# Graph layers on one core: scores of gathered tiles taken earlier and pinned in order, the diagonal's and `mixed`'s evictions moved later

## The chip, the core and the metric

The kernel runs on one core of a Trainium2 chip. The metric is device time in microseconds (us), from the start of the program to its end. One more execution was taken with the hardware profiler; its span and its rows are what is read below. Engines are named as in the profile: PE is TensorE (matrix products), DVE VectorE, ACT ScalarE, POOL GpSimd, SP SyncE. PEld is the loading of weights, beside PE.

## The reference

There are 64 graphs of 256 nodes with 256 features, and all share one weighted adjacency matrix `adj` (256 x 256, about 3% of it not zero, symmetric in its pattern, with a full diagonal). Four layers follow each other: 0, 1 and 3 are of one kind, and 2 is attention. The weights differ from layer to layer.

```python
def gnn(h, adj, W1, b1, W2, b2, Wa, ba, Wm, bm, beta1, beta2, beta3):   # layers 0, 1, 3
    pre_u = einsum('bud,dk->buk', h, W1[:d])
    pre_v = einsum('bvd,dk->bvk', h, W1[d:])
    hidden = relu(pre_u[:, :, None, :] + pre_v[:, None, :, :] + b1)
    S = sigmoid(einsum('buvk,ko->buvo', hidden, W2)[..., 0] + b2[0])
    a = einsum('buv,bud->bvd', S * adj, h)
    m = einsum('uv,bud->bvd', adj, h) * h
    return beta1 * h + beta2 * (a @ Wa + ba) + beta3 * (m @ Wm + bm)

def attention(x, adj, W1, W2, b2, bias2):                               # layer 2
    feats = einsum('bni,oi->bno', x, W1)
    f1 = einsum('bno,o->bn', feats, W2) + b2[0]
    coefs = softmax(leaky_relu(f1[:, :, None] + f1[:, None, :]) + adj, axis=-1)
    return einsum('bij,bjo->bio', coefs, feats) + bias2 + x
```

The score `S[u, v]` is wanted only where `adj[u, v]` is not zero. For each such edge it is a sum over 256 features of `relu(pre_u[u] + pre_v[v] + b1) * W2`.

## The kernel before, in words

**Edges in slots.** The edges off the diagonal are put into 16 blocks of 128 slots, and what does not fit goes into a rest (`left`). A block is named (k, m, i): half k of row block m, quarter i of the columns. For each slot the row pre_u[u] + pre_v[v] + b1 is wanted, for two graphs g at once. It comes in one of three ways.

- Eight blocks (`FAST`) are *made* by TensorE: `pick` (a 0/1 matrix) times `pre` (copies of rows of `pu` and `pv` that ScalarE lays out, `rows_u` L751 and `rows_v` L760), into one of three PSUM tiles `ga` (L697).
- Eight blocks (`FETCHED`) and `left` are *gathered* by POOL's indirect DMAs (L742, in the order `FETCHES`). SP first writes `pu` and `pv` as tables to DRAM (L630). For each block one gather takes the rows of `tableu`, and a second one adds those of `tablev` on top. A stage has 18 gathers. The first six (`AHEAD`) are issued in `before`, the others in `scores`.
- The diagonal (u = v) needs no gather: `own` is pu + pv, added by DVE out of PSUM (L636, four 128x256 adds a stage).

**Scores.** `rated` is one DVE instruction per block and graph (L661, tile `junk`): relu, times W2, summed to a column of `raw`. `rated_all` then turns a run of columns into scores on ACT (tanh at L681, an add of 1 at L682), and four DVE products write them as matrices `rm` (L689). It is called twice a stage: for `EARLY` (the rest, the diagonal and all blocks of m = 0, with the product `ro` for the rest on ACT, L684) and for `LATE` (all blocks of m = 1, in `end`, when all else of the stage is issued).

**Back to the graph.** `early` makes the matrix `sa` from the diagonal and the rest: PE products of `ro` and `guo` (L771) into two PSUM tiles, and four DVE steps (L775). `spread` adds the blocks: for m = 0 and then m = 1, PE products of `rm` and `gu` (L787) and one DVE add (L789). `finish` then has the products `sa,h` (L281, evicted to `aT` by ACT, L344), those with the weights Wm and Wa (L366, or L352 in the last layer), DVE's sum into `hT` or `h` (L369, L356), and transposes (L287). `mixed` has the products `adj,h` (L281) and DVE's products with `hT` into `mT` (L316). `before` has the products of `hT` with W1 (L625), `pu` on ACT (L626) and `pv` on DVE (L627). `attention` has products with `qb` (L401) and `w2q` (L407), the exponentials `e` on ACT, transposes of `e` that ACT copies to SBUF (`ident,e`, L287), and the products `f,logits` (L448).

**Two streams.** Stream a has 16 pairs of graphs, stream b the other 16. While the scores of one stream's layer are taken (the *heavy* side), the other stream does all its work between two score phases (the *light* side): `after` (= `spread` and `finish`), attention if it is due, and `before` of the next layer, which ends with `mixed`. `beside` weaves them: the light side is a generator, and with each step it yields a number p, or a pair (p, f): so many made tiles, and so many steps of `got` (gathered tiles), are issued there. `REST_OF_IT` issues all that remains, so everything from there on (`early`, L771) stands at the end of the stage, just before `mixed`'s `adj,h`.

**Stages.** There are 96 score phases. Six make a cycle for four graphs: the scores are those of layer 0 of a, layer 0 of b, layer 1 of a, layer 1 of b, layer 3 of a, layer 3 of b, and attention is on the light side of the fourth and the fifth. Where the text cuts a stage at the first `adj,h` matmul, the `LATE` rating and `spread` of the scores just finished fall into the first microseconds of the next stage.

**What sets the order.** A tile scheduler orders each engine's instructions by a model of when their operands come; `tc.issue_after(x)` makes an instruction stand behind x on its engine. Before the change it is used for the gathers (each behind the last) and for the rows of `pre` (behind the last stage's rating, `past`). PSUM has five `ps` tiles for everything but `ga`.

Of the kernel before, what the change touches and what calls it, by code (L numbers as in the profile page):

```python
# [9 lines left out]
FP = mybir.dt.float32  # L10
# [5 lines left out]
P = 128  # L16
# [16 lines left out]
FAST = [(0, 0, 2), (0, 0, 3)] + [(0, 1, i) for i in range(4)] + [(1, 0, 2), (1, 0, 3)]  # L33
# [4 lines left out]
FETCHES += [(-1, 0), (2, 1), (4, 0), (3, 1), (5, 0), (-1, 1), (6, 0), (4, 1), (7, 0), (5, 1), (6, 1), (7, 1)]  # L38

AHEAD = 6  # L40

# [16 lines left out]
def quarter(q):  # L58
    return slice(q * 64, (q + 1) * 64)

# [18 lines left out]
def adj_seq_kernel(ctx: ExitStack, tc: tile.TileContext, a: dict, out: bass.AP):  # L79
# [15 lines left out]
    mm = nc.tensor.matmul  # L95
# [36 lines left out]
    def z_weights(l):  # L132
        for kept, n, beta in ((wm, "Wm", "beta3"), (wa, "Wa", "beta2")):
            kept[l] = const.tile([P, 2, D], FP, name=l + n)
            nc.sync.dma_start(out=kept[l], in_=a[l + n].rearrange("(c p) e -> p c e", p=P))
            nc.scalar.mul(kept[l], kept[l], sca(l + beta))
        zbias[l] = const.tile([P, 2], FP, name=l + "zbias")
        zb = const.tile([P, 2], FP, name=l + "zb")
        nc.vector.tensor_scalar(zb, vecs[:, VEC[l + "ba"], :], sca(l + "beta2"), None, ALU.mult)
        nc.vector.scalar_tensor_tensor(  # L140
# [5 lines left out]
    for l in GNN:  # L146
        halfb2[l] = const.tile([P, 1], FP, name=l + "halfb2")
        nc.vector.tensor_scalar(halfb2[l], sca(l + "b2"), 0.5, None, ALU.mult)
    twob2 = const.tile([P, 1], FP, name="twob2")
    nc.vector.tensor_scalar(twob2, sca("L2_gnn_b2"), 2.0, None, ALU.mult)  # L150
# [7 lines left out]
    def counts(keep, pool, pc):  # L158
# [3 lines left out]
        nc.vector.tensor_scalar(mask, adj, 0.0, None, ALU.not_equal)  # L162
# [6 lines left out]
        nc.vector.tensor_tensor_scan(upto.rearrange("p s v -> p (s v)"), flat, flat, 0.0, ALU.add, ALU.bypass)  # L169
        past = pool.tile([P, 8], FP, name="past")  # L170
        nc.vector.memset(past, 0.0)
        nc.vector.tensor_copy(past[:, 1:8], upto[:, 0:7, 63])
        deg = pool.tile([P, 8], FP, name="deg")
        nc.vector.tensor_tensor(deg, upto[:, :, 63], past, ALU.subtract)
# [17 lines left out]
        nc.vector.tensor_copy(first, t[:, 0:8])  # L192
        last = keep.tile([P, 8], FP, name="last")
        nc.vector.tensor_tensor(last, first, deg, ALU.add)

        over = pool.tile([P, 8], FP, name="over")
        nc.vector.tensor_scalar(over, t[:, 8:16], -128.0, 0.0, ALU.add, ALU.max)
        begin = keep.tile([P, 9], FP, name="begin")
        nc.vector.memset(begin, 0.0)
        nc.vector.tensor_tensor_scan(begin[:, 1:9], over, over, 0.0, ALU.add, ALU.bypass)  # L200
        t = pc()
        mm(out=t[:, 0:1], lhsT=other, rhs=begin[:, 8:9], start=True, stop=True)
        nc.vector.tensor_scalar(begin, begin, t[:, 0:1], None, ALU.add)
        number = keep.tile([P, 8, 64], FP, name="number")
        shift = pool.tile([P, 8], FP, name="shift")
        nc.vector.tensor_tensor(shift, first, past, ALU.subtract)
        nc.vector.tensor_tensor(number, upto, shift.unsqueeze(2).to_broadcast([P, 8, 64]), ALU.add)
# [752 lines left out]
```

## Time and profile before

| | us |
|---|---|
| median of 3 runs | 3524.88 |
| lowest, highest | 3524.08, 3527.32 |
| the profiled execution, its own time | 3531.84 |
| its span, first to last instruction | 3529.9 |
| PE busy | 3446.7 |
| DVE busy | 2605.4 |
| POOL busy | 2227.1 |
| ACT busy | 1599.5 |
| granted TensorE clock, mean | 0.992 |

The busy times are sums over instructions. A matmul's record ends at a modelled time, so PE's busy time also covers short holes between matmuls; where a hole matters, the starts of the records are compared. A 512-column product in fp32 shows as two records, and so on; the counts behind an x are records. In the waits, "PE ps L787 <- DVE rm L689: 29.4, 31, 4.9" reads: PE waited before L787 for a DVE instruction of L689, 29.4 us in all, 31 times, 4.9 at the longest.

### The profile page before, as it was taken

To read this page: it belongs to the slowest core of one execution; us is meant where nothing else is said; L and a number is where in the kernel's file an instruction comes from. 1 tells how busy PE (TensorE), PEld (TensorE's weight loads), DVE (VectorE), ACT (ScalarE), POOL (GpSimd) and SP (SyncE) were. 2 spreads that over 40 slices of the span, in tenths; PEclk is the share of its full clock that TensorE was granted. 3 is DMA by queue.
4 is the path that set the end of the run, shared out by engine and by line. 5 is a ranking of instruction groups with operands and counts; after the bars stand their busy time and mean duration, and the time that the engine had idled before them with its cause. 6 is when DMAs were issued, how large, how long until landed. Compare 5 with 4: busy or idle time off the path is not lost.

```text
span 3529.9 us, 48385 instructions
## 1 busy us (share of the span) xinstructions
PE 3446.7 (98%) x14328; PEld 2106.0 (60%) x14328; DVE 2605.4 (74%) x10584; ACT 1599.5 (45%) x2929; POOL 2227.1 (63%) x1754
## 2 busy tenths in 40 slices
PE   6999999999999999999999999999999999999998
PEld 3566565656656566565666656556565665656655
DVE  5777686777867777777777777768677787777776
ACT  2444444444444444444545445444444444444452
POOL 3747667576665757667576675766757566675754
PEclk7999999999999999999999999999999999999999
DMA  5768777687777867778687776867768677786865
GB/s 148 163 141 192 155 178 168 160 182 155 182 157 170 176 146 188 150 181 181 145 191 161 178 172 151 188 153 185 163 162 179 150 187 157 176 177 146 192 150 114
DMA packets 274733, 587.25 MB, mean 166 GB/s; under 512 B 37024, under 2 KB 54304, under 8 KB 274464
## 3 DMA queue, kind: packets, MB, share of 16 engines
q0 software_dynamic: 190464, 427.93, 60.7%
q1 hardware_dynamic: 82416, 154.96, 12.7%
q8 instruction: 116, 1.90, 0.2%
q10 hardware_dynamic: 1584, 1.20, 0.1%
q14 instruction: 153, 1.25, 0.1%
HBM read 466.51 MB, written 117.44 MB: 165 GB/s over the span
## 4 chain that ended last, share of the span: by engine, by line
PE 72%; DVE 11%; DMA 5%; POOL 5%; issue 5%; ACT 2%; ACTq 0%; POOLq 0%; DVEq 0%
PE ga L697 14%; PE ps L281 13%; PE ps L625 13%; PE ps L366 10%; PE ps L352 5%; POOL fetched L742 4%; PE ps L787 4%; PE ps L448 3%; DVE junk L661 3%; PE ps L407 3%; DMA fetched<-tablev,ids_v 3%; DVE rm L689 3%; PE ps L287 2%; DVE sa L775 2%; PE ps L401 2%
## 5 line engine op out<-in xcount | busy, mean ns | idle before, releaser
L742 POOL DMA_INDIRECT fetched<-tablev,ids_v x768 | 1210.7, 1576 | 355.3 <-issue 232.6
L742 POOL DMA_INDIRECT fetched<-tableu,ids_u x768 | 764.8, 996 | 824.1 <-DMA tableu<-pu 594.0
L697 PE MATMUL ga<-pre,pick 128*128 128x512 f32 x1536 | 769.7, 605 | 11.7 <-DVE junk L661 8.4
L625 PE MATMUL ps<-L_gnn_w,hT 128*128 128x512 f32 x1536 | 695.5, 596 | 5.8 <-DMA hT<-in_xT_dram 5.8
L661 DVE SCALAR_TENSOR_TENSOR junk<-ga,L_gnn_w2row 128x256 f32<-128x256 f32 x1536 | 582.7, 418 | 134.6 <-PE ga L697 122.6
L661 DVE SCALAR_TENSOR_TENSOR junk<-fetched,L_gnn_w2row 128x256 f32<-128x256 f32 x1536 | 595.1, 417 | 35.1 <-DMA fetched<-tablev,ids_v 35.0
L760 ACT COPY pre<-pv 64x512 f32<-64x512 f32 x768 | 473.5, 616 | 108.8 <-DVE pv L627 86.7
L625 PEld LDWEIGHTS ps<-L_gnn_w,hT 128*128 128x128 f32 x1536 | 285.1, 191 | 334.7 <-issue 313.6
L751 ACT COPY pre<-pu 64x1024 f32<-64x1024 f32 x384 | 392.9, 1039 | 3.9
L369 DVE TENSOR_TENSOR hT<-hb,ps 128x512 f32<-128x512 f32 x128 | 88.0, 687 | 412.9 <-PE ps L366 412.9
L697 PEld LDWEIGHTS ga<-pre,pick 128*128 128x128 f32 x1536 | 274.7, 191 | 179.2 <-issue 122.4
L281 PE MATMUL ps<-adj,h 128*128 128x256 f32 x1536 | 358.7, 386 | 11.1 <-DVE own L636 8.0
L281 PE MATMUL ps<-sa,h 128*128 128x256 f32 x1536 | 362.4, 385 | 3.7 <-issue 2.9
L281 PEld LDWEIGHTS ps<-sa,h 128*128 128x128 f32 x1536 | 290.3, 192 | 109.0 <-issue 46.2
L626 ACT COPY pu<-ps 128x256 f32<-128x256 f32 x384 | 142.4, 371 | 466.9 <-PE ps L625 443.2
L281 PEld LDWEIGHTS ps<-adj,h 128*128 128x128 f32 x1536 | 283.4, 190 | 80.0 <-issue 36.8
L330 ACT ACTIVATE hb<-hT,L_gnn_zbias,scas 128x512 f32<-128x512 f32 x128 | 97.4, 807 | 450.3 <-DVE hT L369 356.7
L689 DVE TENSOR_TENSOR rm<-gva,val 128x256 f32<-128x256 f32 x768 | 279.0, 417 | 9.7 <-ACT val L682 7.2
L787 PEld LDWEIGHTS ps<-rm,gu 128*64 128x64 f32 x3072 | 172.4, 137 | 139.2 <-PE ps L281 55.4
L787 PE MATMUL ps<-rm,gu 128*64 128x128 f32 x3072 | 215.9, 280 | 30.9 <-DVE rm L689 29.4
L344 ACT COPY aT<-ps 128x512 f32<-128x512 f32 x192 | 112.6, 586 | 293.2 <-PE ps L281 250.3
L366 PE MATMUL ps<-mT,L_gnn_Wm 128*128 128x512 f32 x512 | 240.6, 592 | 0.0
(155 smaller groups left out, 4200.2 us busy)
## 6 DMA issues: line engine op xcount, KB each, us to landing
tableu<-pu SPq DMA_DIRECT2D x192, 256.0 KB
tablev<-pv SPq DMA_DIRECT2D x192, 256.0 KB
hT<-in_xT_dram SPq DMA_DIRECT2D x32, 512.0 KB
h<-in_x_dram SPq DMA_DIRECT2D x64, 256.0 KB
out_dram<-h SPq DMA_DIRECT2D x64, 256.0 KB
fetched<-tableu,ids_u POOLq DMA_INDIRECT x768
fetched<-tablev,ids_v POOLq DMA_INDIRECT x768
L_gnn_w<-in_L_gnn_W_dram SPq DMA_DIRECT2D x6, 256.0 KB
```

The lines of the kernel that those rows point to most:

```text
L281: mm(out=o[:, m, :], lhsT=lhs[:, c, blk(m)], rhs=rhs[:, c, :], start=c == 0, stop=c == 1)
L352: mm(out=z[:, m, :], lhsT=y[:, c, g, blk(m)], rhs=w[:, c, :], start=j == 0 and c == 0, stop=j == 1 and c == 1)
L366: mm(out=z, lhsT=w[:, c, blk(m)], rhs=y[:, c], start=j == 0 and c == 0, stop=j == 1 and c == 1)
L625: mm(out=t, lhsT=hT[:, c, g, blk(m)], rhs=w1[l][:, c], start=c == 0, stop=c == 1)
L626: nc.scalar.copy(pu[:, m, g, :], t[:, 0, :])
L661: nc.vector.scalar_tensor_tensor(junk, t, 0.0, w2row[l], ALU.max, ALU.mult, accum_out=raw[:, i : i + 1])
L689: nc.vector.tensor_tensor(rm[:, k, ms, g, :], gva[:, k, ms, :], val[:, i : i + 4].unsqueeze(2).to_broadcast([P, 4, 64]), ALU.mult)
L697: mm(out=t, lhsT=pick[:, k, 4 * m + i, :], rhs=pre[:, n], start=True, stop=True)
L742: this = nc.gpsimd.indirect_dma_start(out=to, out_offset=None, in_=rows, in_offset=bass.IndirectOffsetOnAxis(ap=ids, axis=0), compute_op=( ...
L751: nc.scalar.copy(st["pre"][h, f : f + n], st["pu"][h, m].rearrange("p g d -> p (g d)").unsqueeze(1).to_broadcast([64, n, 2 * D]),)
L760: nc.scalar.copy(st["pre"][halves[1 - k], n], st["pv"][halves[i % 2], i // 2].rearrange("p g d -> p (g d)"))
L787: mm(out=t[h, :, quarter(i)], lhsT=gu[:, k, 4 * m + i, :], rhs=rm[:, k, 4 * m + i], start=True, stop=True)
```

## The change

Six things are changed.

1. `FAST` lists all blocks of m = 0 first, so `EARLY` needs only the first four made tiles. The rows of `pre` follow that order.
2. In `FETCHES`, the second gather of `left` goes one place ahead.
3. The step tables are new (`STEPS`, and `steps` in `before`). `early` becomes a step of its own behind the `EARLY` rating, and in the changed kernel's program its matmuls stand in mid-stage. In the last layer the diagonal is a step of its own, at the start.
4. `Noting` keeps the last instruction that was issued on PE, DVE and ACT, and `behind` puts made tiles, scores of gathered tiles, the diagonal's adds, `rated_all`'s tanh and `early`'s instructions behind it on the same engine.
5. `own` is no longer added out of PSUM in `before` but in `itself`, from `pu` and `pv` in SBUF: two 128x512 adds a stage in place of four 128x256.
6. `mixed`'s DVE products into `mT` are kept in a list `later` and issued behind `spread`'s second add, one stage boundary on.

```diff
-FAST = [(0, 0, 2), (0, 0, 3)] + [(0, 1, i) for i in range(4)] + [(1, 0, 2), (1, 0, 3)]
+FAST = [(k, 0, i) for k in range(2) for i in (2, 3)] + [(0, 1, i) for i in range(4)]
...
-FETCHES += [(-1, 0), (2, 1), (4, 0), (3, 1), (5, 0), (-1, 1), (6, 0), (4, 1), (7, 0), (5, 1), (6, 1), (7, 1)]
+FETCHES += [(-1, 0), (2, 1), (4, 0), (3, 1), (-1, 1), (5, 0), (6, 0), (4, 1), (7, 0), (5, 1), (6, 1), (7, 1)]
...
+STEPS = {
+    GNN[0]: [(1, 1), (1, 1), (0, 1), (1, 0), (0, 1), (2, 1)],
+    GNN[1]: [(0, 0), (0, 1), (0, 1), (0, 0), (0, 1), (1, 1), (0, 0), (1, 1)],
+    LAST: [(1, 1), (1, 1), (0, 1), (0, 1), (1, 1), (1, 0)],
+}
...
+class Noting:
+    def __init__(self, engine):
+        self.engine = engine
+
+    def __getattr__(self, op):
+        def issue(*a, **k):
+            self.last = getattr(self.engine, op)(*a, **k)
+            return self.last
+        return issue
...
+    tensor, vector, scalar = Noting(nc.tensor), Noting(nc.vector), Noting(nc.scalar)
+    mm = tensor.matmul
+
+    def behind(engine):
+        return tc.issue_after(engine.last.ins)
...
-        def mixed(st, l):
+        def mixed(st, l, later=None):
...
-                nc.vector.tensor_tensor(mT[:, :, g, :], t, st["hT"][:, :, g, :], ALU.mult)
+                times = (mT[:, :, g, :], t, st["hT"][:, :, g, :], ALU.mult)
+                if later is None:
+                    vector.tensor_tensor(*times)
+                else:
+                    later.append(times)
...
-            got = {LAST: (1, 0, 1, 1), GNN[1]: (1, 1, 1, 1), GNN[0]: (0, 0, 2, 1)}[l]
-            got = dict(zip(order, got))
+            steps = {LAST: [(0, 1), (0, 1), 0, 0], GNN[1]: [0, (0, 1), (0, 1), (0, 1)], GNN[0]: [(0, 1), 0, (0, 1), (0, 1)]}[l]
...
-                nc.vector.tensor_tensor(own[:, m, g, :], t[:, 0, :], pv[:, m, g, :], ALU.add)
-                if g == 1:
-                    if m == 0:
-                        rows_u(st, 0, 2, 0, 0)
-                    rows_v(st, 2 - 2 * m, 2, 0)
-                yield 0, got[(m, g)]
+                if (m, g) == (0, 1):
+                    rows_u(st, 0, 2, 0, 0)
+                    rows_v(st, 4, 2, 0)
+                if (m, g) == (1, 1):
+                    rows_v(st, 0, 2, 0)
+                yield steps[n]
...
-            yield from mixed(st, l)
+            yield from mixed(st, l, later if past else None)
...
             def rated_all(cols, m):
-                nc.scalar.activation(val[:, cols], raw[:, cols], AF.Tanh, bias=halfb2[l], scale=0.5)
+                with behind(scalar):
+                    scalar.activation(val[:, cols], raw[:, cols], AF.Tanh, bias=halfb2[l], scale=0.5)
...
-                    mm(out=t, lhsT=pick[:, k, 4 * m + i, :], rhs=pre[:, n], start=True, stop=True)
+                    with behind(tensor):
+                        mm(out=t, lhsT=pick[:, k, 4 * m + i, :], rhs=pre[:, n], start=True, stop=True)
...
-                    if n < 2:
-                        both(own[:, n], DIAGONAL + 2 * n, DIAGONAL + 2 * n + 1)
+                    count.append(n)
                     yield
...
+            def itself(m):
+                with behind(vector):
+                    vector.tensor_tensor(*(flat(t)[:, m] for t in (own, st["pu"], st["pv"])), ALU.add)
+                both(own[:, m], DIAGONAL + 2 * m, DIAGONAL + 2 * m + 1)
...
             def got(made):
+                if l == LAST:
+                    itself(0)
+                    itself(1)
+                    yield
                 for f, block in enumerate(FETCHED):
                     if f == FIRST:
-                        for _ in made:
-                            yield
-                        rated(left, REST)
+                        while len(count) < 4:
+                            next(made)
+                        with behind(vector):
+                            rated(left, REST)
                         rated_all(EARLY, 0)
                         yield
-                    tile_scores(fetched[f], *block)
-                    if f == FIRST + 1:
                         early(st)
+                        yield
+                    if l != LAST and f < 2:
+                        itself(f)
+                    with behind(vector):
+                        tile_scores(fetched[f], *block)
                     yield
...
         def early(st):
...
-                    mm(out=sides[g][:, m, :], lhsT=guo[h, m, :], rhs=ro[h, :], start=True, stop=True)
+                    with behind(tensor):
+                        mm(out=sides[g][:, m, :], lhsT=guo[h, m, :], rhs=ro[h, :], start=True, stop=True)
...
-                    nc.vector.scalar_tensor_tensor(
+                    with behind(vector):
+                        vector.scalar_tensor_tensor(
...
         def spread(st, l):
...
-                nc.vector.tensor_tensor(sa[:, m], sa[:, m], t, ALU.add)
+                it = vector.tensor_tensor(sa[:, m], sa[:, m], t, ALU.add)
+            with tc.issue_after(it.ins):
+                while later:
+                    vector.tensor_tensor(*later.pop(0))
```

Two step values inside `attention` and the yields of `finish` (now read from `STEPS`) move by one place as well. Elsewhere `nc.vector`, `nc.scalar` and `nc.tensor` become `vector`, `scalar` and `tensor`, which issue the same instructions.

## The prediction, made blind

> **What bounds the kernel.** I read the page's busy line first, then the chain that ended last, then TensorE's waits.
>
> ```profile
> PE 3446.7 (98%) x14328; PEld 2106.0 (60%) x14328; DVE 2605.4 (74%) x10584; ACT 1599.5 (45%) x2929; POOL 2227.1 (63%) x1754
> ...
> PE 72%; DVE 11%; DMA 5%; POOL 5%; issue 5%; ACT 2%; ACTq 0%; POOLq 0%; DVEq 0%
> ```
>
> TensorE is the bound, and the change leaves it the same matmuls. Only time in which it waits can be won. Its waits by the profile:
>
> ```profile
> PE ps L787 <- DVE rm L689: 29.4, 31, 4.9
> PE ga L697 <- DVE junk L661: 8.4, 2, 7.8
> ...
> PE ps L281 <- DVE own L636: 8.0, 5, 2.6
> ...
> PE ps L771 <- ACT ro L684: 3.8, 2, 3.1
> ```
>
> The largest is `spread` (L787) waiting for the rated scores `rm`. Busy 98% hides more than this: a matmul's end is modelled, so short holes show only in the spacing. I therefore cut one cycle of six stages (four graphs; 16 cycles make the run) at the first `adj,h` matmul of each stage. These are the windows, columns as on the page; the last three are granted clock, DMA share and GB/s:
>
> ```profile
> 1575.21:1606.46 31.25, 31.25 (x138) 20.33 (x136) 25.63 (x106) 14.46 (x25) 23.98 (x19) 1.00 0.86 196
> 1606.46:1638.60 32.14, 32.14 (x130) 18.12 (x128) 24.21 (x104) 15.41 (x27) 22.21 (x18) 1.00 0.81 174
> 1638.60:1672.15 33.55, 32.34 (x130) 18.39 (x128) 24.87 (x103) 15.43 (x27) 22.77 (x18) 1.00 0.77 166
> 1672.15:1715.81 43.66, 43.08 (x183) 26.55 (x181) 32.06 (x132) 20.78 (x40) 22.04 (x18) 1.00 0.64 139
> 1715.81:1758.60 42.79, 42.79 (x182) 26.21 (x180) 32.05 (x128) 19.85 (x40) 22.68 (x19) 1.00 0.67 154
> 1758.60:1789.51 30.91, 30.91 (x139) 20.49 (x137) 22.31 (x88) 13.54 (x25) 23.71 (x20) 1.00 0.88 206
> ```
>
> I call them stages 0 to 5. Matmuls that follow without a wait are 0.429 us apart with 512 columns, 0.216 with 256. Summed so, the stages would take 30.16, 30.98, 30.98, 41.39, 41.39 and 30.16. They lose 1.1, 1.2, 2.6, 2.3, 1.4 and 0.75 us. Stage 5 waits for nothing, so about 0.75 (1.16 in the attention stages 3 and 4) is the cost of switching between operand kinds. What is left is about 5 us a cycle, and it lies in the second half of `spread`:
>
> ```profile
> 1643.11 1.09 PE L787 MATMUL ps<-rm,gu 128*64 128x128 f32 x16
> 1645.42 1.42 PE L787 MATMUL ps<-rm,gu 128*64 128x128 f32 x16 [1.21 <-DVE rm L689]
> ```
>
> ```profile
> 1763.11 1.97 PE L787 MATMUL ps<-rm,gu 128*64 128x128 f32 x32
> ```
>
> ```profile
> 1794.02 1.09 PE L787 MATMUL ps<-rm,gu 128*64 128x128 f32 x16
> 1795.04 1.98 PE L697 MATMUL ga<-pre,pick 128*128 128x512 f32 x4
> 1796.95 1.09 PE L787 MATMUL ps<-rm,gu 128*64 128x128 f32 x16
> ```
>
> Stage 2 (first fence) takes 3.66 us from the first half to the next matmul, stage 5 (second) 1.97. In stages 0 and 1 (third) the scheduler has put four made tiles between the halves: no wait, but two more switches, and the second half starts only 7.44 us into the stage.
>
> **The change, part by part.** (1) `early` leaves the stage's end. Its eight matmuls took 1.06 us there (1757.54 to 1758.60) between the last L625 and `adj,h`, and its four `sa` steps 1.64 us of VectorE at the next stage's start. Both go to mid-stage. TensorE does them all the same, so this saves nothing directly. It takes the `sa` steps (and the two `own` evictions, 0.74 us, and the two `mT` evictions, 1.3 us) from in front of `rm`. It also brings the stage's start 1.06 us closer to the table writes, so every gather of the next stage lands 1.06 us later as the stage counts.
>
> (2) With `rm` sooner in VectorE's order, the program of the changed kernel has both halves of `spread` together in all six stages, after the 16 `adj,h` records and one made tile (two records). Stage 5's row puts the first half at 1763.11 - 1758.60 = 4.51 us, so the second needs `rm` at 4.51 + 1.02 = 5.53. Mean gains over the cycles, read as above: stage 0 0.41 and stage 1 0.45 (no split), stage 2 2.35 (all its excess, with the `adj,h` wait for `own`), stage 3 1.06, stage 4 0.25. Sum 4.52.
>
> (3) What is late next is the last gathered tile. Chain from its landing: two `junk` at 0.345 (the spacing of 1641.88 and 1642.22), tanh and add about 0.6, four `rm` 1.42: 2.7 us. So it must land by 5.53 - 2.7 = 2.8 us into the next stage. The trace has stage 5's last landing 33.78 us after that stage's start, 2.88 into stage 0; with the shift of (1) 3.95. Ready at 6.65, against a need of 5.53: a new wait of 1.1 us in stage 0, up to 1.4 if a `junk` of another tile stands before it. I take 1.25. Before, the split hid this, as 7.44 was late enough. Why stage 5 cannot start its gathers sooner is in POOL's rows: from the table write to the next stage they follow each other without a hole.
>
> ```profile
> 1784.49 1.56 POOL L742 DMA_INDIRECT fetched<-tablev,ids_v  x1 [0.30 <-issue]
> 1786.35 1.54 POOL L742 DMA_INDIRECT fetched<-tablev,ids_v  x1 [0.30 <-DMA fetched<-tableu,ids_u]
> 1788.20 0.99 POOL L742 DMA_INDIRECT fetched<-tableu,ids_u  x1 [0.30 <-issue]
> ```
>
> Nine gathers at 1.28 and nine at 1.86 us make 28.3 us of a stage of 30.9. The same sum for the other boundaries: stage 0's last lands 33.34 - 31.25 + 1.07 = 3.2 into stage 1, less the 1 us by which stage 0 is now longer: 2.2. Stage 1's comes 33.47 - 32.14 + 1.07 = 2.4 into stage 2, less some 0.5: 1.9. Stage 2's comes 32.54 - 33.55 + 1.07 + 2.35 = 2.4 into stage 3. They fit, by 0.6, 0.9 and 0.4 us. Stages 3 and 4 have over 7 us.
>
> (4) In mid-stage `early` waits for `left`: its second gather, one place sooner (1.28 us), lands near 22.7 us in stage 0. Order and landing are close; I take 0.15 us there, between 0 and 0.6.
>
> (5) Attention. In stage 4, three made tiles (2.57 us) stood between the last `w2q` matmul and `ident,e`, whose `e` was ready 2.24 us after it. Now two stand there, 1.72: a wait of 0.5. In stage 3, `f,logits` waits for ScalarE's copy (0.59) that now queues behind the other graph's two exponentials: 0 to 0.9, I take 0.86.
>
> (6) `own` as one SBUF add for each m: 384 evictions of 0.41 us (157.5) become 192 adds of 0.61 to 0.68 (117 to 131) by the 128x512 rows. VectorE is 74% busy, so I count nothing; without that cover it would be a gain of 0.3 us a stage. The deferred `mT` holds two of five PSUM tiles about 4 us longer; the next taker is `sa,h`, behind `spread`, so nothing. Table writes on SP are not moved. The pins are order only; ahead of a pinned `junk` that waits for its landing, though, VectorE holds back all that is queued behind it.
>
> The new add reads two SBUF operands. By the Trainium skill ("SBUF — State Buffer", "Who interferes with whom") such an instruction keeps GpSimd from reading SBUF until it ends. If that held for the gathers' issue, two adds of 0.68 a stage would put 1.4 us on POOL's queue, and stages 0 to 3 would pay 1.4, 0.8, 0.5 and 1.0: the sum would be +1.9 a cycle, 3556 us. The trace speaks against it: `junk<-fetched`, 1536 of them with two SBUF operands, runs beside a queue whose rows keep 0.30 us apart.
>
> Sum a cycle: -4.52 + 1.25 + 0.15 + 0.5 + 0.86 = -1.76. Times 16: -28.2 us. In the last stage of the run, which has no other stream beside it, L787 waits 6.2 of its 29.4 us; that hangs on the last landing and stays, so 0 (between -3 and +3). The profiled execution took 3531.84 us (span 3529.9, so 1.9 lie around it); it would take 3503.6. It stands 7.0 above the median of the three runs, so 3497.
>
> **Rivals.** A, the full gain: the last landing is no later than before (the scheduler's stage starts shift less than I count) and attention hides its waits. Then -4.52 x 16 = -72, 3453; halfway is 3475. For: the margins in (3) and (5) are under a microsecond. Against: POOL's queue has no room in stages 5, 0 and 1.
>
> B, slower: the chain from landing to `rm` is longer by d in every stage, because pinned scores hold VectorE for a tile that has not come and `pv` or `hT` come late behind them. Stage 0 pays d, stages 1, 2 and 3 d less 0.6, 0.9 and 0.4. It decides from -1.76 + 4d - 1.9 = 0, d = 0.92. At d = 1.5 it is +2.34 x 16 = +37: 3562. For: `junk L661 <- DMA fetched` already waited 35.0 us on VectorE, and pins forbid filling such holes. Against: 3.7 us of VectorE work leave the front of the same queue.
>
> C, the gain goes to attention: both waits of (5) at twice my size, 1.36 more: -0.4 x 16 = -6, 3519.
>
> D, nothing: the order is set by data and the pins change no start, 3525. Against: in the changed kernel's program L787 and `early` stand elsewhere.
>
> **Numbers.** My sum 0.45, A 0.15, B 0.25, C 0.1, D 0.05. A run of this kernel can be told from no change from about 0.2%, 7 us: faster is below 3517.8, slower above 3531.9. Faster: my sum, A, and some of C, 0.62; same 0.08; slower 0.30, B with the upper part of mine. The range goes from halfway to A and a little beyond, 3457, to B with d = 1.15, 3540.
>
> **What would show it.** Right: L787 as x32 in every stage; the wait of L787 gone from stages 2 and 3 and a new one of about 1.2 us in stage 0 alone; stage 2 near 31.2 us, stage 0 near 32.3; `ident,e` waits 0.5 us in stage 4. Wrong: L787 waits at the start of stages 1 to 3 as well (B); `junk L661 <- DMA fetched` far over 35 us; POOL's gathers further apart than 0.30; a stage 0 below 31 us (A).

## The result, and the profile after

The changed kernel took 3547.65 us (median of 4, 3544.06 to 3548.77), beside 3526.1 for the kernel before (3524.08 to 3527.94): a ratio of 1.0052, 95% interval 1.0036 to 1.0069. The forecast was 3497, with a range to 3540. So it is slower, by 18 us (the ratio) to 22 us (the medians), where a gain of 28 was forecast. A ratio in this text is not quite that of the two medians beside it; the two differ by up to 0.15%.

The page after; its busy line and the chain:

```profile
span 3547.0 us, 48320 instructions
...
PE 3438.4 (97%) x14328; PEld 2119.6 (60%) x14328; DVE 2638.9 (74%) x10392; ACT 1627.5 (46%) x2929; POOL 2254.0 (64%) x1754
...
PE 70%; DVE 8%; POOL 7%; DMA 7%; issue 6%; ACT 2%; another core or an unknown queue 0%; POOLq 0%; ACTq 0%; DVEq 0%
```

The chain has given DVE's share (11% to 8%) to POOL and DMA (5% and 5% to 7% and 7%): along it, scores wait less for VectorE and more for gathers. TensorE's waits say what replaced what. All engine lines are now L76 (the helper that notes instructions), so tiles tell them apart:

```profile
PE ps L76 <- DVE rm L76: 33.4, 17, 8.5
PE ps L76 <- ACT logits L76: 14.1, 15, 1.2
PE ps L76 <- DVE sa L76: 13.6, 17, 1.5
...
PE ps L76 <- ACT e L76: 5.8, 18, 0.3
```

The wait of `spread` for `rm` is not smaller (29.4 before), but it comes 17 times and not 31. New are 14.1 us before `f,logits`, 13.6 before `sa,h` and 5.8 before `ident,e`. The windows of one cycle, stages 0 to 5 (columns as in the prediction):

```profile
1365.90:1399.00 33.10, 31.45 (x138) 20.65 (x137) 25.30 (x104) 14.76 (x25) 24.34 (x19) 1.00 0.83 190
1399.00:1430.85 31.85, 31.85 (x130) 18.43 (x128) 25.42 (x106) 15.35 (x26) 22.12 (x18) 1.00 0.80 177
1430.85:1462.54 31.69, 31.69 (x130) 18.28 (x128) 24.39 (x98) 15.73 (x27) 23.56 (x19) 1.00 0.76 173
1462.54:1506.47 43.93, 42.84 (x182) 26.46 (x180) 32.83 (x130) 20.30 (x40) 24.16 (x18) 1.00 0.62 133
1506.47:1551.41 44.94, 43.05 (x182) 26.40 (x181) 32.74 (x126) 20.29 (x40) 23.00 (x18) 1.00 0.64 147
1551.41:1582.77 31.36, 31.31 (x137) 20.55 (x136) 22.14 (x82) 14.79 (x26) 23.97 (x19) 1.00 0.86 213
```

The change of each stage against before, means over 14 cycles, in us. The last column is e5 below, the same kernel on another chip.

| stage | forecast | first profile | e5 |
|---|---|---|---|
| 0 | +1.00 | +1.82 | +1.50 |
| 1 | -0.45 | -0.37 | -0.31 |
| 2 | -2.35 | -2.08 | -2.00 |
| 3 | -0.20 | +0.47 | 0.00 |
| 4 | +0.25 | +1.35 | +0.33 |
| 5 | 0 | +0.25 | +0.15 |
| cycle | -1.76 | +1.43 | -0.33 |

Sixteen times +1.43 is +23; the span grew by 17.2 (the start and the first six stages are 7.7 us shorter, the run's end 4.8 longer, and 14 cycles 20.0 longer). Four places carry it.

**Stage 0, the last landing.** PE, then DVE:

```profile
1370.30 1.09 PE L76 MATMUL ps<-rm,gu 128*64 128x128 f32 x16
1373.04 1.42 PE L76 MATMUL ps<-rm,gu 128*64 128x128 f32 x16 [1.65 <-DVE rm L76]
1374.40 1.98 PE L76 MATMUL ga<-pre,pick 128*128 128x512 f32 x4
```

```profile
1370.49 0.42 DVE L76 SCALAR_TENSOR_TENSOR junk<-fetched,L_gnn_w2row 128x256 f32<-128x256 f32 x1 [1.35 <-DMA fetched<-tablev,ids_v]
...
1371.89 1.43 DVE L76 TENSOR_TENSOR rm<-gva,val 128x256 f32<-128x256 f32 x4 [0.62 <-ACT val L76]
```

VectorE waits 1.35 us for the last tile, then come two `junk`, tanh and add (a gap of 0.62) and `rm`; TensorE stands for 1.65. This is the wait that the prediction named, only longer.

**Stage 3, the copy of eT.** ScalarE takes the second graph's two exponentials, whose `top` was late, ahead of the copy that `f,logits` needs:

```profile
1492.20 0.91 ACT L76 ACTIVATE e<-logits,top 128x256 f32<-128x256 f32 x2 [1.13 <-DVE top L76]
1493.01 0.56 ACT L76 COPY logits<-ps 128x512 f32<-128x512 f32 x1
```

```profile
1493.63 2.01 PE L76 MATMUL ps<-f,logits 128*128 128x258 f32 x8 [1.09 <-ACT logits L76]
```

**Stage 4, `ident,e`** loses 0.57 in every cycle (forecast 0.5).

**Stage 4, the late completion.** This was not in the prediction:

```profile
1510.87 2.12 PE L76 MATMUL ps<-rm,gu 128*64 128x128 f32 x32
1512.92 1.12 PE L76 MATMUL ga<-pre,pick 128*128 128x512 f32 x2
1513.88 0.60 PE L76 MATMUL ps<-sa,h 128*128 128x256 f32 x2
1516.02 1.78 PE L76 MATMUL ps<-sa,h 128*128 128x256 f32 x7 [1.54 <-DVE sa L76]
```

```profile
1513.04 0.69 DVE L76 TENSOR_TENSOR sa<-sa,ps 128x512 f32<-128x512 f32 x1 [0.50 <-PE ps L76]
1515.28 0.69 DVE L76 TENSOR_TENSOR sa<-sa,ps 128x512 f32<-128x512 f32 x1 [1.55 <-PE ga L76]
```

Both halves of `spread` were issued without a hole and should have ended by 1511.97 and 1512.99, but the semaphore events of the trace that release the two `sa` adds come at 1513.02 and 1515.26: 1.0 and 2.3 us late. VectorE has nothing else in front, so it waits, and `sa,h` with it. In the kernel before, at the same place of a stage 4, other scores stand in front of `sa`:

```profile
1722.07 0.42 DVE L661 SCALAR_TENSOR_TENSOR junk<-own,L_gnn_w2row 128x256 f32<-128x256 f32 x1
...
1722.42 1.28 DVE L789 TENSOR_TENSOR sa<-sa,ps 128x512 f32<-128x512 f32 x2
```

I measure this below by the mean time that `sa` in stage 4 starts later than both the modelled end of its matmuls and the end of the instruction before it: 0.62 us here, -0.08 in the kernel before.

### The profile page after: what moved, and what is told of

The parts are those of the page before. It is cut to its first block, busy times and chain, and to the rows that moved or that the text cites. A ratio compares the mean times of both kernels' runs of the same rounds, so it can differ in the third digit from the quotient of the medians.

```text
span 3547.0 us, 48320 instructions
## 1 busy us (share of the span) xinstructions
PE 3438.4 (97%) x14328; PEld 2119.6 (60%) x14328; DVE 2638.9 (74%) x10392; ACT 1627.5 (46%) x2929; POOL 2254.0 (64%) x1754
## 4 chain that ended last, share of the span: by engine, by line
PE 70%; DVE 8%; POOL 7%; DMA 7%; issue 6%; ACT 2%; another core or an unknown queue 0%; POOLq 0%; ACTq 0%; DVEq 0%
PE ps L76 57%; PE ga L76 13%; POOL fetched L785 6%; DMA fetched<-tablev,ids_v 5%; DVE junk L76 3%; DVE rm L76 1%; POOL left L785 1%; DVE e L76 1%; DMA tableu<-pu 1%; ACT e L76 1%; DVE sa L76 1%; DMA fetched<-tableu,ids_u 1%; ACT logits L76 1%; DVE logits L76 0%; ACT val L76 0%
## 5 line engine op out<-in xcount | busy, mean ns | idle before, releaser
L785 POOL DMA_INDIRECT fetched<-tablev,ids_v x768 | 1224.9, 1595 | 347.5 <-issue 245.5
L785 POOL DMA_INDIRECT fetched<-tableu,ids_u x768 | 772.4, 1006 | 821.2 <-DMA tableu<-pu 590.4
L76 PE MATMUL ga<-pre,pick 128*128 128x512 f32 x1536 | 778.6, 603 | 4.6 <-DVE junk L76 4.6
L76 PE MATMUL ps<-L_gnn_w,hT 128*128 128x512 f32 x1536 | 701.5, 598 | 5.8 <-DMA h<-in_x_dram 5.8
L76 DVE SCALAR_TENSOR_TENSOR junk<-fetched,L_gnn_w2row 128x256 f32<-128x256 f32 x1536 | 584.7, 420 | 152.5 <-DMA fetched<-tablev,ids_v 146.8
L76 DVE SCALAR_TENSOR_TENSOR junk<-ga,L_gnn_w2row 128x256 f32<-128x256 f32 x1536 | 585.3, 419 | 98.9 <-PE ga L76 91.1
L76 ACT COPY pre<-pv 64x512 f32<-64x512 f32 x768 | 473.5, 616 | 64.5 <-DVE pv L76 47.0
L76 PEld LDWEIGHTS ps<-L_gnn_w,hT 128*128 128x128 f32 x1536 | 284.6, 191 | 333.8 <-issue 302.9
L76 ACT COPY pre<-pu 64x1024 f32<-64x1024 f32 x384 | 391.8, 1044 | 7.4
L76 PE MATMUL ps<-sa,h 128*128 128x256 f32 x1536 | 365.7, 382 | 14.1 <-DVE sa L76 13.6
L76 PEld LDWEIGHTS ga<-pre,pick 128*128 128x128 f32 x1536 | 277.6, 191 | 165.2 <-issue 131.9
L76 PEld LDWEIGHTS ps<-sa,h 128*128 128x128 f32 x1536 | 289.9, 191 | 132.6 <-issue 55.9
L76 DVE TENSOR_TENSOR rm<-gva,val 128x256 f32<-128x256 f32 x768 | 275.3, 421 | 126.0 <-ACT val L76 115.0
L76 DVE TENSOR_TENSOR pv<-ps,L_gnn_b1row 128x256 f32<-128x256 f32 x384 | 162.4, 423 | 266.2 <-ACT pu L76 264.3
L76 PE MATMUL ps<-adj,h 128*128 128x256 f32 x1536 | 347.4, 379 | 0.6 <-DVE pv L76 0.6
L76 ACT COPY pu<-ps 128x256 f32<-128x256 f32 x384 | 143.0, 372 | 439.2 <-PE ps L76 420.4
L76 PEld LDWEIGHTS ps<-adj,h 128*128 128x128 f32 x1536 | 291.8, 190 | 81.6 <-issue 34.7
L76 ACT ACTIVATE hb<-hT,L_gnn_zbias,scas 128x512 f32<-128x512 f32 x128 | 97.3, 806 | 464.7 <-DVE hT L76 383.4
L76 PEld LDWEIGHTS ps<-rm,gu 128*64 128x64 f32 x3072 | 178.6, 138 | 115.0 <-issue 61.0
L76 PE MATMUL ps<-rm,gu 128*64 128x128 f32 x3072 | 210.3, 280 | 33.7 <-DVE rm L76 33.4
L76 PE MATMUL ps<-mT,L_gnn_Wm 128*128 128x512 f32 x512 | 240.6, 592 | 0.0
L76 PE MATMUL ps<-aT,L_gnn_Wa 128*128 128x512 f32 x512 | 240.6, 592 | 0.0
```

Of the source, the lines that this page charges most:

```text
L76: self.last = getattr(self.engine, op)(*a, **k)
L785: this = nc.gpsimd.indirect_dma_start(out=to, out_offset=None, in_=rows, in_offset=bass.IndirectOffsetOnAxis(ap=ids, axis=0), compute_op=( ...
```

## The experiments

Every edit is on the changed kernel, and every ratio is to the kernel before on the same chip. Runs of one group (e1 to e4, e5 to e8, e9 to e12, e13 to e16, e17 and e18) shared a chip; between groups compare stages, not microseconds.

**e1.** LATE's tanh no longer pinned: `-with behind(scalar):` `+with behind(scalar) if m == 0 else nullcontext():`

> The changed kernel, with only the LATE rating's tanh no longer pinned behind the last instruction on ScalarE; its program then has it ahead of the rows of pre. Theory P (the pin is a cost of its own): in stages 4 and 5 the tanh stops waiting for rows of pre that wait for pv, rm is ready some 2 us sooner, sa,h's loss in stage 4 falls from 0.95 to about 0.25 us, spread's in stages 4 and 5 from 0.31 to 0.15: about -1.0 us a cycle, -16 us, near 3531. Rival L (only the last landing counts): in the long stages the tiles have landed long before, so nothing moves, 3547 within 4; stage 0 stays at about 33.1 in both.

3531.62 us, ratio 0.9987 (0.9978 to 0.9997). `spread`'s loss falls from 0.31 to 0.15 in stages 4 and 5, as P has it: 0.3 us a cycle. The rest of what I expected in stage 4 (0.95 at `sa,h`) is gone in e2 to e4 too, which do not touch it. By these two stages the pin costs 5 us, not 16.

**e2.** Two made tiles between the halves in stage 0:

```diff
                 it = vector.tensor_tensor(sa[:, m], sa[:, m], t, ALU.add)
+                if m == 0 and l == LAST and st["side"] == "b":
+                    yield 2
...
```

> The changed kernel, with two made tiles put back between the two halves of spread in stage 0 alone. Theory L (in stage 0 the second half comes 1.9 us too soon for the last gathered tile): spread's loss in stage 0 falls from 2.27 to about 0.15, 0.4 comes back for the split: -1.7 us a cycle, -27 us, near 3520. Rival G (the made tiles' scores queue on VectorE behind the same pinned landing, so the hole only moves to ga): less than 8 us won, and PE ga waits for DVE junk in stage 0.

3533.58 us, 0.9997 (0.9986 to 1.0008). Stage 0 is 33.0 (32.8 in e5), so no gain, but not for G's reason:

```profile
PE ga L76 <- ACT pre L76: 17.8, 15, 3.3
```

The made tiles wait for rows of `pre`, which are pinned behind the LATE rating (`past`), which waits for the same landing. In the kernel before, the piece that the second tile there needs was 1.04 us of ScalarE (rows of `pu`); the new order of `FAST` makes it 2.3 (rows of `pv` too), behind a landing that is 1.2 us later.

**e3.** One more made tile ahead of `ident,e`: `-yield 1, g` `+yield 2 - g, g`

> The changed kernel, with attention's first step back at two made tiles (three between w2q and ident,e, as before the change). Theory A (the step tables cost the attention stages): ident,e's loss in stage 4 falls from 0.57 to 0, and the 1.12 us ahead of the made tile and f,logits in stage 3 to about 0.3, since 0.86 us more lie ahead of the copy of eT: -1.4 us a cycle, -22 us, near 3525. Rival Q (the copy of eT is late because ScalarE takes both graphs' exponentials first, whatever TensorE does): stage 3 keeps its 1.1, only 0.57 goes, -9 us, near 3538.

3543.73 us, 1.0033 (1.0021 to 1.0044). Rival Q: stage 3 keeps 1.28 ahead of `f,logits` and loses 0.89 more behind the second `ident,e`, where the next `f,logits` waits for its copy; only stage 4's 0.57 goes.

**e4.** `early` called just before `mixed` again:

```diff
                         rated_all(EARLY, 0)
                         yield
-                        early(st)
                         yield
...
             yield REST_OF_IT
+            if at_end:
+                at_end.pop()()
             yield from mixed(st, l, later if past else None)
...
```

> The changed kernel, with early's matmuls and its four sa steps back at the end of the stage; pins, orders, own and mT as changed. Theory L: the stage start is 1.06 us later against the gathers again, so stage 0 wins 1.06 (-17 us), but four sa steps (1.64 us) stand in front of rm again and spread waits up to 0.5 us more in stages 1, 2 and 3 (up to +24): between -10 and +10 in sum. Rival M (early's place is most of what the change wins in stages 1 and 2): +30 us or more, stages 1 and 2 back above 32.5 and 33.5 us. Rival N (early's place is what loses): -25 us or more.

3568.33 us, 1.0093 (1.0068 to 1.0117), 35 to 37 us above its neighbours e2 and e1. M's size, but not its place: stages 1 and 2 are 32.3 and 31.75; stage 0 grows to 34.5, as the four `sa` steps are in the way of `rm` there. The first gather of stage 5 does go out 1.1 us sooner by the stage's count (0.56 against 1.66), but the last one lands no sooner (4.2 into stage 0 both times).

**e5.** The changed kernel, unedited, on a second chip.

> The changed kernel itself, once more, as the anchor for the runs beside it. In its first profile spread's second add (sa) came up to 2.3 us after spread's matmuls in stages 2 to 5, and sa,h waited 0.95 us in stage 4; four variants that leave that place alone show none of it. Theory X (it belongs to that one run or chip): sa,h in stage 4 loses under 0.3 us, stage 4 takes 43.2, and the ratio to the kernel before is about 1.001 to 1.003. Rival Y (it belongs to the program): stage 4 at 44.1 again and the ratio at 1.005.

3513.15 us, 0.9995 (0.9986 to 1.0004). Stage 4 takes 43.13, and `sa` follows at once:

```profile
1488.09 2.12 PE L77 MATMUL ps<-rm,gu 128*64 128x128 f32 x32
1490.13 1.13 PE L77 MATMUL ga<-pre,pick 128*128 128x512 f32 x2
1491.10 3.62 PE L77 MATMUL ps<-sa,h 128*128 128x256 f32 x16
```

```profile
1489.67 1.28 DVE L77 TENSOR_TENSOR sa<-sa,ps 128x512 f32<-128x512 f32 x2
```

So without late completions the change is worth nothing either way: the gain of stages 1 and 2 (2.3 us a cycle) goes to stage 0 and a little to 4 and 5.

**e6.** All of attention's yields as before the change (`2 - g`, `1`, `0`).

> The changed kernel with all yields of attention as before the change: the gathered tiles' steps leave attention, so early goes behind it in stages 3 and 4. Theory A (early and the exponentials of the second graph in front of the copy of eT cost stage 3): the 1.1 to 1.25 us ahead of f,logits in stage 3 fall under 0.3, ident,e's 0.57 in stage 4 goes; -1.5 us a cycle, -24 us against e5. Rival Q (the copy of eT stands behind both graphs' exponentials in any case): only ident,e's 0.57, -9 us or less.

3541.99 us, 1.0072 (1.0059 to 1.0085). Neither theory had the sum right. The hole before the first `f,logits` closes and `ident,e`'s 0.57 in stage 4 goes, as A has it, but 0.89 is lost behind the second `ident,e` in stages 3 and 4, and with the gathered tiles' steps gone from attention the LATE scores come late: `spread` loses 1.12 in stage 4 and 1.80 in stage 5. The new steps are a gain of 0.8% over the old ones in the changed kernel.

**e7.** Two products with W1 ahead of `spread` in stage 0: `halfway(after(...), 4, ...)` becomes `halfway(after(...), 1 if side == "b" else 4, ...)`

> The changed kernel with the first two products of the next pair with W1 (L625 of before, 3.43 us of TensorE, no new work) moved ahead of spread in stage 0 alone. They need no gathered tile, no row of pre and no score. Theory L (stage 0's second half of spread is 1.1 to 2.2 us ahead of the last gathered tile, and that is the main loss): spread's loss in stage 0 falls from 2.3 to about 0.3, stage 0 from 33.2 to 31.3; -1.9 us a cycle, -30 us against e5. Rival G (the landing only moves on to the next stage, since POOL's queue is full from stage 5 to stage 1): stage 0 wins 1.9 but stage 1 loses 1 or more of it; -14 us or less.

3518.25 us, 1.0000 (0.9990 to 1.0009). Beside e5, stage 0 wins 0.15 and stage 1 loses 0.41. TensorE now waits for PSUM:

```profile
PE ps L76 <- DVE pv L76: 14.3, 15, 1.6
```

`pv`, which frees the products' tiles, stands on VectorE behind the pinned scores that wait for the landing and behind `rm`, and two of the five tiles are held by the deferred `mT`.

**e8.** e7 with e1.

> e7 and e1 together: the W1 products ahead of spread in stage 0, and the LATE tanh not pinned. If the two costs are separate (theory L with P) the gains add: spread's loss in stage 0 near 0.3 and in stages 4 and 5 at 0.15, about 5 us below e7. Rival: ScalarE's order is one queue, the free tanh moves ahead of the rows of pre in stage 0 too and the made tiles wait for those; no better than e7 within 3 us.

3511.03 us, 0.9986 (0.9977 to 0.9994), 7 us under e7. The free tanh adds to it as expected.

**e9.** e2, and the first rows of `pre` not pinned in any stage: `-if past else` `+if past and n else`

> The changed kernel with e2's split (two made tiles between the halves of spread in stage 0) and, in every stage, the first piece of the rows of pre no longer pinned behind the LATE rating of the stage before. In e2 the made tiles in the hole waited for just those rows (PE ga for ACT pre, 17.8 us). Theory R (that pin is why the split won nothing): ga's loss in stage 0 falls from 1.7 to 0.3, stage 0 from 32.9 to 31.6; near 20 us under the changed kernel on the same chip, a ratio near 0.994 to 0.996. Rival V (VectorE, in order and pinned behind the landing, holds the made tiles' scores and so the three ga tiles): ga waits for DVE junk instead and stage 0 stays over 32.5.

3562.76 us, 1.0080 (1.0060 to 1.0100). R holds in stage 0 (31.73, and no wait at `ga`). But in the others the still pinned tanh now queues behind those rows: `spread` loses 0.67, 0.98, 0.86, 1.28 and 1.28 in stages 1 to 5.

**e10.** Scores of gathered tiles and of `left` not pinned.

> The changed kernel with the scores of gathered tiles and of left no longer pinned on VectorE; the scheduler places them. Theory B (the pins hold VectorE behind tiles that have not come): the wait of junk for landings falls from 147 us to under 60, and the run by 10 us or more. Rival L (the landing itself is late, whoever waits): the wait moves to other instructions and the run stays within 5 us; if the scheduler puts the scores later than the pins do, rm comes later and stages 0 to 3 grow by 0.5 us or more each (+30 us).

3590.52 us, 1.0142 (1.0108 to 1.0176). The other way round from theory B:

```profile
DVE junk L76 <- DMA fetched<-tablev,ids_v: 278.3, 227, 3.7
```

The wait nearly doubles (146.8 in the first profile, with the pins): left to itself, the scheduler puts scores even further ahead of their landing. Stage 1 grows to 34.6, and over the run PE waits 28.3 us for `pv`. The pins help.

**e11.** `own` added out of PSUM in `before` again.

> The changed kernel with own added out of PSUM again in before (four 128x256, one SBUF operand), its scores where the change puts them. Theory F (own is free either way): within 5 us; POOL's gathers stay at 1006 and 1595 to 1606 ns. Rival S (an add with two SBUF operands holds up POOL): POOL's rows go back to 996 and 1576 ns, the last landing comes 0.2 us sooner or more and stage 0 with it: -4 us or more.

3551.01 us, 1.0049 (1.0032 to 1.0067). On this chip the changed kernel was not run; late completions are as in its first profile (0.65 in stage 4), and so is the ratio. This fits F, as far as ratios from two chips can tell. The gathers take 999 and 1585 ns here, against 1006 and 1595 in the first profile and 1008 and 1599 in e9 on this chip: 0.2 us a stage, and stage 0 (33.67) is no sooner. The Trainium skill's rule ("SBUF — State Buffer", "Who interferes with whom") of an add with two SBUF operands that keeps GpSimd from reading SBUF does not show as the 1.4 us a stage that it would be at its worst.

**e12.** `mT` evicted at once: `mixed(st, l)` without `later`.

> The changed kernel with mT evicted at once in mixed, as before the change. Theory D (the later eviction wins the front of VectorE's queue for rm): 1.3 us stand in front of rm again; in stages 1 to 3, where rm is ready 0.1 to 0.6 us before it is wanted, spread waits 0.7 to 1.2 us more: +2.5 us a cycle, +35 us or so. Rival H (VectorE idles there until the landing, and mT fits in the hole): under 5 us, and a gain where PSUM was short.

3559.73 us, 1.0060 (1.0036 to 1.0083), 9 us above e11 by the medians, though the two intervals overlap. D in direction: `spread` loses 0.9 in stages 4 and 5, where e11 has 0.3. But `sa` follows its matmuls again in stage 4 (0.07 against 0.65 on the same chip), so the two nearly cancel. The completions themselves are still late: the semaphore event of the first half comes 0.37 to 1.11 us after the modelled end in all 14 cycles, that of the second half 0.2 to 0.5 us in 13. One `mT` step again stands among the `rm` steps, and VectorE reaches the first `sa` no sooner than its event.

**e13.** The changed kernel a third time, on the chip of e1 to e4.

> The changed kernel on the chip of these runs. Theory X (late completions make the difference between chips): where sa comes late after spread in stages 2 to 5 by more than 0.5 us in the mean of stage 4, the ratio to before is 1.004 to 1.006; where it does not, 0.998 to 1.001. Rival Z (the chips differ in the gathers alone): the ratio goes with the landing in stage 0, and the sa rows are the same in both.

3570.19 us, 1.0106 (1.0089 to 1.0123). `sa` in stage 4 is 0.93 late and `sa,h` loses 1.59. Theory X: one and the same program gives 0.9995, 1.0052 and 1.0106 where `sa` in stage 4 is -0.08, 0.62 and 0.93 us late, and the last landing is 4.1 to 4.2 us into stage 0 each time. It is not the chip as such, since e1 to e4 on this chip have none of it. The wait it makes here, in the whole run:

```profile
PE ps L77 <- DVE sa L77: 21.6, 19, 2.3
```

The kernel before does not show it: on this chip it took 3533.1 us beside e1 to e4 and 3535.0 beside e13 to e16.

**e14.** e2's split, rows of `pre` free in stage 0's scores alone, tanh free.

> The changed kernel with the split of spread in stage 0 (e2), the first rows of pre not pinned behind the last rating in stage 0's scores alone (e9 did it in all stages and lost in 2 to 5), and the LATE tanh free (e1). Theory R: stage 0 falls from about 33 to 31.7, stages 4 and 5 by 0.15 each: -1.5 us a cycle, 20 to 27 us under e13. Rival V: what the rows take on ScalarE delays the free tanh, and stage 1 gives back what stage 0 wins: within 8 us of e13.

3553.26 us, 1.0061 (1.0043 to 1.0079), 17 us under e13. Stage 0 falls to 32.1 (33.2 in e13), but stage 1 rises by 0.8 (its `spread` loses 1.2): the shorter stage only brings the next one closer to its own last landing. V in kind. Most of the 17 us stands elsewhere, in stage 4 (0.7 us a cycle), where `sa,h` loses 0.6 less although `sa` is as late as in e13; the edit was not meant for that place.

**e15.** A second made tile between `spread` and `sa,h` in stages 3 and 4: `-yield 1 if l == GNN[1] else 2` `+yield 2`, and one less in `STEPS`.

> The changed kernel with a second made tile between spread and sa,h in the attention stages 3 and 4 (taken from later in the same stage; no new work). Theory X: on a chip with late completions sa,h's loss in stage 4 falls from 0.95 to 0.2 and in stage 3 from 0.2 to 0: -12 to -15 us against e13; on a chip without them nothing, within 4 us. Rival Z: within 4 us on both, or slower where the tile is missed later.

3554.63 us, 1.0060 (1.0043 to 1.0077), 15.6 us under e13. `sa` is as late as in e13 (0.86), but `sa,h` loses 0.82 and not 1.59. X.

**e16.** e14 and e15.

> e14 and e15 together. If the two losses are separate the gains add: about 20 to 27 us under e13 on a chip without late completions, 32 to 42 on one with them. Rival: the made tiles are eight a stage and each can cover only one place; no better than e14.

3542.62 us, 1.0020 (1.0009 to 1.0030), 27.6 us under e13. Most of both (17 and 15.6).

**e17.** The order of the gathers alone:

```diff
-FETCHES = [(0, 0), (1, 0), (2, 0), (0, 1), (3, 0), (1, 1)]
+FETCHES = [(0, 0), (1, 0), (2, 0), (3, 0), (0, 1), (1, 1)]
```

> The changed kernel with the first gathers of four blocks issued ahead of the first second gather (three before), so that POOL's wait of about 2 us for the first landing is filled with one issue of 1.28 us. Theory L (POOL's full queue from stage 5 to stage 1 sets the last landing): it comes 1.2 us sooner in stages 5, 0 and 1; spread's loss in stage 0 falls from 2.1-2.3 to about 1.0, in stage 1 from 0.4-0.5 to 0.2; -1.4 us a cycle, 22 us under the changed kernel in a like session (a ratio of 0.993 where that has 0.9995, 1.004 where it has 1.0106). Rival T (the landings are set by the tables or by the transfers themselves): the wait only moves along the queue, the last landing stays within 0.3 us and the time within 5 us of the changed kernel.

3500.71 us, **0.9902 (0.9887 to 0.9917)**. This beats the kernel before, measured on the same chip; the changed kernel was not run there. Stages 0, 1 and 2 win together (32.08, 31.82 and 31.69 against e5's 32.82, 31.94 and 32.12), and stages 3 to 5 stay as they are. Only e6 had all three clearly shorter too, and it lost 3.0 us in stages 4 and 5. POOL's wait, in the changed kernel and in e17, at the same place of a stage 0:

```profile
1368.47 1.13 POOL L785 DMA_INDIRECT fetched<-tableu,ids_u  x1 [0.30 <-issue]
1371.96 1.79 POOL L785 DMA_INDIRECT fetched<-tablev,ids_v  x1 [2.36 <-DMA fetched<-tableu,ids_u]
```

```profile
1771.51 1.18 POOL L785 DMA_INDIRECT fetched<-tableu,ids_u  x1 [0.30 <-issue]
1773.34 1.71 POOL L785 DMA_INDIRECT fetched<-tablev,ids_v  x1 [0.66 <-DMA fetched<-tableu,ids_u]
```

The last tile of stage 5 lands 34.33 us into its stage against 35.27 in e5. Over the run POOL's wait falls from 106.8 to 64.2 us, first the changed kernel, then e17:

```profile
POOL fetched L785 <- DMA fetched<-tableu,ids_u: 106.8, 99, 3.2
```

```profile
POOL fetched L785 <- DMA fetched<-tableu,ids_u: 64.2, 97, 2.4
```

This run has no late completions (-0.08), so its gain is to be held against e5's 0.9995. The two ratios are 33 us apart; the stages explain 1.3 us a cycle, 21 us of it.

**e18.** e17 with e1 and e15.

> e17 with the LATE tanh free (e1) and one more made tile between spread and sa,h in stages 3 and 4 (e15). If the three are separate: 0.25 us a cycle from the tanh, up to 0.7 from the made tile where completions come late, 1.4 from the gathers; 26 to 36 us under the changed kernel, so below the kernel before in a session without late completions (a ratio near 0.992) and near or below it in one with them (0.998 to 1.003). Rival: what e17 wins is taken back where the made tile is missed later; no better than e17.

3505.98 us, 0.9922 (0.9908 to 0.9935). The rival: no better than e17. Stage 0 gives back 0.7 and the tanh wins 0.3; there was no late completion to cover. Why stage 0 does, the runs leave open: POOL waits as little as in e17 (64.0 us), but the scores of the last tile start 4.25 us into stage 0 in the mean, as in e5 (4.30), and not at 3.57 as in e17.

## Why the prediction was wrong, step by step

**The gains of step (2)** were nearly right. In stage 2 `spread` and `adj,h` gave 2.0 of 2.35 us, in stage 1 0.3 to 0.4 of 0.45 came; in stage 3 `spread`'s loss fell from 1.21 to 0.19, the 1.0 that was forecast. L771 in mid-stage, and both halves of L787 without a wait between them in stages 3, 4 and 5 always and in 1 and 2 in most cycles: as said.

**Step (3), "I take 1.25", is the term that was mis-sized.** The landing itself was close: 4.2 us into stage 0 for 3.95. The chain of 2.7 was right too (second half at 6.9 in e5). Left out were that a half which starts after a stop takes 1.42 and not 1.09 (the rows above), and the scatter of the landings: the mean loss at `spread` came to 1.9 us in e5 and 2.1 in the first profile. What made it dear is that nothing could stand in its place: e2, e7 and e14 show made tiles, PSUM and the next stage each tied to the same landing. I had the reason in sight ("they follow each other without a hole") and read it too well: the queue had one hole in each stage, at the fourth gather of the list. In e5 it is 2.3 and 2.5 us in stages 0 and 1 and 0.6 to 1.2 in the others, where 0.30 is usual. With it filled (e17) POOL is through with stage 5's gathers 0.76 us sooner and the landing comes 0.9 sooner. That the hole alone set the landing is not shown, since e18 has it filled as well and its stage 0 is as long as e5's.

**Step (4)** put 0.15 at `early` in stage 0. Nothing was lost there in the first profile and in e5, 0.16 in e3: within its range.

**Step (5)** was right in both terms: 0.57 for 0.5, and 1.0 to 1.1 for 0.86, for the cause given. C's doubling did not come from there.

**Step (6), "the pins are order only"**, failed in a small way: tanh behind the rows of `pre` costs `spread` 0.16 in stages 4 and 5 each (e1). Where it feared the pins, at scores that wait for a landing, they were worth their price (e10). `own` was free as far as e11 tells, `mT` later was a gain of 0.6 in stages 4 and 5 each (e12).

Together the mis-sized terms come to 1.43 us a cycle, 23 us of the run (-1.76 forecast, -0.33 in e5): 0.50 in stage 0, 0.35 in stage 2, 0.20 in stage 3, the rest in the others. They alone take the gain away.

**What no step had** is the late completion. Between e5 and the first profile lie 1.76 us a cycle, 28 us of the run. Of these 1.3 us, 21 of the 28, are lost at `sa,h` in stages 3 to 5; the rest is scattered, most of it at `spread` in stage 0 and `f,logits` in stage 3. This is what turned nothing into a loss. Clearing VectorE's queue was meant to bring `rm` forward; it also left `sa` with nothing to hide a late matmul. In the kernel before, the event of the first half comes 0.3 to 0.4 us late in 7 of the 9 stages 4 where it is recorded (5.98 for 5.60), and the `junk` and `own` scores that stood ahead of `sa` covered it. That covering was a cost of the old order that I counted as waste only.

**The rivals.** B had the sign, but not the mechanism: stages 1 and 2 did not pay, and the chain was not longer. One of its signs came true: `junk`'s wait for landings rose from 35.0 to 146.8 us. It cost TensorE little outside stage 0, where nearly all of `spread`'s wait for `rm` is. The right rival would have been "the cover is gone", asked of `sa` as it was asked of `rm`.

**Left open.** Why the matmuls of `spread` are reported late. It goes by groups of runs and not by the program. All ten traces of three groups have it, whatever their edit: the two kernels' first profiles, e9 to e12, and e13 to e16. In the ten traces of the other groups (e1 to e4, e5 to e8, e17 and e18) the events recorded for `spread` in stage 4 come within 0.03 us of the modelled end, but for one of 0.22. The ten late traces also hold a fifth fewer semaphore events, 37,864 to 39,574 against 48,829 to 48,942, for nearly the same instructions. VectorE's late starts do not rest on those events, as its instructions have records of their own. Whether both have one cause is not known, and no variant was run in a group of each kind but the changed kernel itself.

## What to carry to other kernels

When a wait is taken away in front of an instruction, ask of the next one what its own producer's latest time is, not its mean: work that stood in the way may have been its cover. And where a queue is full over several stages, fill its own holes (e17: one line, 0.9902 of the kernel before where the changed kernel had 0.9995) before work is moved under its landings, since in e7 and e14 that only handed the wait to the next stage. A kernel that has to be judged within 1% should be run on more than one chip and more than once on a chip: the same program stood at 0.9995 and at 1.0106 of the kernel before.

## What the runs showed of the hardware that was not expected

A matmul's completion can reach VectorE up to 2.3 us after the matmul should have ended by the profile, while TensorE goes on issuing; in some groups of runs this happens in most cycles at the same instruction (19 waits of `sa,h`, 21.6 us, in e13), in others, with the same program, never (e5).

The 16 records of a half of `spread` take 0.33 us longer when they start after a stop (1.42 against 1.09). A gather that adds to the result of one before it holds POOL until that one has landed, 4 to 6 us after its issue. Behind three first gathers, 1.28 us apart, that left a hole of 2.36 us in the stage 0 shown, and behind four 0.66.
